# Moving the steps of a slot: places for convolution, attention and routing among the last convolution's products

## The chip, the cores and the metric

The kernel runs on one core of one Trainium2 chip. The metric is the device time of one execution in microseconds, the median of several; lower is better. The core has a matrix engine (TensorE, PE in the profile, with its weight loads as PEld), VectorE (DVE), ScalarE (ACT), GpSimd (POOL), and SyncE (SP), which here only issues transfers. Each engine works off its own list of instructions in order, and the lists meet at semaphores.

## The reference

The model has three parts on an image batch of 8 x 56 x 56 x 256 floats.

```python
# 32 paths: 1x1 convolution to 4 channels, 3x3 convolution, 1x1 back to 256, each with
# batch norm and relu; the paths are summed
paths = jax.vmap(_path, in_axes=(None,) + (0,) * 18)(x, W1, B1, ...)
x = relu(paths.sum(axis=0) + x)
# attention without softmax, per image, on normalised tokens; k and v are normalised per head
kv = einsum('bhnd,bhne->bhde', k, v) / N
out = einsum('bhnd,bhde->bhne', q, kv)
t = t + out + ln(t)
# 8 experts, 2 for each token, over the normalised tokens
logits = tokens @ router_w.T ; rw, re = top_k(softmax(logits), 2)
out = tokens + sum over e of combine[:, e] * (gelu(tokens @ w1[e] + b1[e]) @ w2[e] + b2[e])
```

## The kernel before, in words

The 8 images are cut into 7 chunks each of 448 tokens (8 rows of the image), so there are 56 chunks. The last loop of the kernel walks through 65 slots `s`. In slot `s` several stages of different chunks are worked on side by side, as in a software pipeline:

- the last convolution of chunk `s` (`conv3_steps`): 16 steps of two products. One product (`pair`, L588) is two matmuls into two PSUM banks; ScalarE makes the relu of one bank (L593), VectorE joins the other bank to it (L596). After every second step TensorE sums four of the results over the paths (`sum_paths`, L609).
- the first convolution of chunk `s + 2` (`conv1_steps`): two turns of the input (L249), then the product (L260) whose result ScalarE writes into the image `h1` (L263).
- the second convolution of chunk `s + 1`: `spread_taps` copies shifted rows of `h1` by 12 transfers into `R` (L284); `conv2_steps` has three rows of taps (L298), all into one PSUM bank, and then `halves`, which splits the result in two parts and moves them to `hl` by 16 transfers (L321), the input of the next slot's last convolution.
- the end of chunk `s - 1` (`end_steps`): relu (L644), turn back to tokens (L656), head means (L668), centring on GpSimd (L682), squares on ScalarE (L691), variances on VectorE with a power on GpSimd (L720), inverses on VectorE (L728), scaling on GpSimd (L738), and the head products (L748).
- the attention of chunk `a = s - 8` (`attn_steps`): four matmuls with VectorE work (L874, L878), a power on GpSimd (L892), means (L896), the normalised payload on ScalarE (L903), and its addition and transfer out (`base`, L933 and L935). At the first chunk of an image `image_steps` first makes the tables (L782 and on). `fetch` loads chunk `a + 1` back from DRAM.
- routing of one or two finished chunks (`route_steps`): a series of small VectorE operations with one power on GpSimd (L1010) up to the rows (L1053 to L1062), then 8 scatters for each chunk from GpSimd's queue (L1065). Each scatter waits for the newest product that was written down before it (`pace`), so that the scatters are spread over the slot. From time to time `plan_steps` works out the next tiles of the experts (L1160 to L1213).
- tiles of the experts (`moe_steps`): turn (L1279), first product and gelu (L1321, L1325), second product (L1337, L1341, L1345), and an indirect add into the output from GpSimd (L1359).

Slots 0 to 7 have no attention yet, slots 8 to 55 have all stages except that the expert tiles begin at slot 17, and slots 56 to 64 have only the rest of the attention and the experts.

What a slot's order is, is settled by `issue`. A stage is given as a stretch from `low` to `high` of the slot and a list of steps with costs; each step gets the place where the middle of its cost falls in the stretch. All steps of all stages are sorted by place and written down in that order. The last convolution takes the whole slot, 0 to 1, so that a place is at the same time a place among its products. For TensorE, VectorE and ScalarE the order of writing is the order of execution. Instructions of GpSimd and SyncE are put in order by the framework's scheduler, from the same program.

PSUM tiles of all stages come from one pool of 7 banks in rotation (`ps_mm`); the path sums have the eighth bank.

## Time and profile before

| what | value |
|---|---|
| time, median of 3 | 3348.13 us (3347.52 to 3353.67) |
| profiled run, span | 3349.9 us |
| TensorE busy | 3002.3 us, 90% |
| VectorE busy | 2196.5 us, 66% |
| ScalarE and GpSimd busy | 1900.6 us and 1903.3 us, 57% each |
| mean granted TensorE clock | 0.955 |
| L596 on VectorE | 1792 times, 676 ns each |
| L593 on ScalarE | 1792 times, 636 ns each |
| first product of slot 0 | 58.5 us after the start |
| last product of slot 55 | 2821.0 us |

A row of the profile's groups gives the line, the engine, the operation, what it writes and reads with the shape, how often, busy time and mean; after the bar the idle time of the engine just before these instructions, and what ended most of it. In a timeline a row begins with the start and the duration in microseconds, and the brackets at its end hold the idle time before it and what ended it. An idle engine costs something only where another engine waits for what it was to do.

### The profile page before, as it was taken

To read this page: it belongs to the slowest core of one execution; us is meant where nothing else is said; L and a number is where in the kernel's file an instruction comes from. 1 tells how busy PE (TensorE), PEld (TensorE's weight loads), DVE (VectorE), ACT (ScalarE), POOL (GpSimd) and SP (SyncE) were. 2 spreads that over 40 slices of the span, in tenths; PEclk is the share of its full clock that TensorE was granted. 3 is DMA by queue.
4 is the path that set the end of the run, shared out by engine and by line. 5 is a ranking of instruction groups with operands and counts; after the bars stand their busy time and mean duration, and the time that the engine had idled before them with its cause. 6 is when DMAs were issued, how large, how long until landed. Compare 5 with 4: busy or idle time off the path is not lost. (4 is left out here: it accounts for less than half of the span.)

```text
span 3349.9 us, 55292 instructions
## 1 busy us (share of the span) xinstructions
PE 3002.3 (90%) x16677; PEld 1686.8 (50%) x16677; DVE 2196.5 (66%) x5881; ACT 1900.6 (57%) x3827; POOL 1903.3 (57%) x1372
## 2 busy tenths in 40 slices
PE   5888888888998999999998999999999998798798
PEld 2333433333444554545455555455545545586677
DVE  3666777777777767776776767777777686344300
ACT  2655555645665665566665666566655665354345
POOL 3222234554456466566656566657565666777677
PEclk7999888989999999999998999999999999899999
DMA  6432234435565675666666677566666665798797
GB/s 153 116 87 73 80 111 127 125 108 147 142 163 158 167 189 157 169 161 180 166 167 171 156 196 184 153 177 174 176 164 167 165 168 156 191 267 218 194 220 177
DMA packets 341482, 537.72 MB, mean 161 GB/s; under 512 B 59952, under 2 KB 251584, under 8 KB 341184
## 3 DMA queue, kind: packets, MB, share of 16 engines
q1 hardware_dynamic: 257088, 429.93, 44.1%
q0 software_dynamic: 81984, 103.45, 16.8%
q8 instruction: 134, 2.20, 0.3%
q14 instruction: 164, 1.34, 0.1%
q10 hardware_dynamic: 2112, 0.81, 0.1%
HBM read 248.01 MB, written 192.55 MB: 132 GB/s over the span
## 5 line engine op out<-in xcount | busy, mean ns | idle before, releaser
L596 DVE SCALAR_TENSOR_TENSOR r<-c,nb,r 128x448 f32<-128x448 f32 x1792 | 1127.1, 676 | 563.1 <-ACT r L593 539.7
L593 ACT ACTIVATE r<-c,b3t 128x448 f32<-128x448 f32 x1792 | 1033.1, 636 | 364.1 <-PE c L588 361.7
L1359 POOL DMA_INDIRECT out_dram<-y,index x420 | 662.3, 1577 | 354.0 <-ACT y L1345 251.2
L588 PE MATMUL c<-hl,W3hl 64*128 64x448 f32 x3584 | 708.9, 429 | 74.0 <-ACT r L593 39.6
L609 PE MATMUL su<-r,gather 128*32 128x448 f32 x3584 | 583.7, 577 | 64.0 <-DVE r L596 63.4
L1065 POOL DMA_INDIRECT regions<-pay,rrowi x448 | 431.8, 964 | 316.8 <-PE c L588 202.5
L588 PEld LDWEIGHTS c<-hl,W3hl 64*128 64x128 f32 x3584 | 343.3, 189 | 509.2 <-issue 209.3
L1321 PE MATMUL ph<-eT,w 128*128 128x256 f32 x1680 | 462.1, 406 | 31.5 <-ACT hT L1325 17.1
L1345 ACT ACTIVATE y<-py,g 128x256 f32<-128x256 f32 x420 | 195.4, 474 | 442.2 <-PE py L1341 329.3
L1341 PE MATMUL py<-w,hT 128*128 128x256 f32 x1680 | 436.9, 385 | 0.2
L720 POOL TENSOR_TENSOR hsd<-hsd,half 112x36 f32<-112x36 f32 x56 | 351.5, 6277 | 79.5 <-DVE hsd L719 79.0
L1321 PEld LDWEIGHTS ph<-eT,w 128*128 128x128 f32 x1680 | 302.9, 196 | 172.0 <-issue 65.8
L1325 ACT ACTIVATE hT<-ph,w 128x256 f32<-128x256 f32 x420 | 197.1, 479 | 258.0 <-PE ph L1321 140.9
L1341 PEld LDWEIGHTS py<-w,hT 128*128 128x128 f32 x1680 | 293.4, 193 | 29.8 <-ACT hT L1325 1.4
L682 POOL TENSOR_TENSOR norm<-t,hmean 112x512 f32<-112x512 f32 x112 | 120.3, 1133 | 329.6 <-PE c L588 181.3
L874 PE MATMUL at<-tab,tT 128*112 128x272 f32 x896 | 263.3, 417 | 4.7 <-ACT r L593 4.4
L609 PEld LDWEIGHTS su<-r,gather 128*32 128x32 f32 x3584 | 104.3, 110 | 272.7 <-DVE r L596 155.0
L1337 PE MATMUL py<-b2hl,own 128*128 128x256 f32 x420 | 178.1, 424 | 20.4 <-ACT y L1345 7.1
L874 PEld LDWEIGHTS at<-tab,tT 128*112 128x112 f32 x896 | 147.8, 180 | 83.2 <-issue 16.7
L298 PE MATMUL c<-R,W2t 96*32 96x448 f32 x1344 | 183.2, 573 | 2.9 <-DMA R<-h 1.8
L903 ACT ACTIVATE pay<-X,nm,rs 112x256 f32<-112x256 f32 x224 | 134.9, 604 | 52.6 <-DVE nm L896 52.6
L1010 POOL TENSOR_TENSOR rq<-ebase,rq 112x8 f32<-112x8 f32 (+1 forms) x32 | 53.0, 1656 | 196.1 <-DVE rq L1009 196.1
(255 smaller groups left out, 3196.9 us busy)
## 6 DMA issues: line engine op xcount, KB each, us to landing
w<-Wd SPq DMA_DIRECT2D x210, 513.0 KB
rows<-regions SPq DMA_DIRECT2D x210, 259.0 KB
xi<-in_x_dram SPq DMA_DIRECT2D x56, 448.0 KB
hl<-hi SPq DMA_DIRECT2D x448, 56.0 KB
tTs<-u SPq DMA_DIRECT2D x56, 448.0 KB
ts<-t SPq DMA_DIRECT2D x56, 448.0 KB
tT<-tTs SPq DMA_DIRECT2D x56, 448.0 KB
X<-ts SPq DMA_DIRECT2D x56, 448.0 KB
```

Source lines behind the costliest of these rows:

```text
L588: product = nc.tensor.matmul(tiles[g][:, :CH], W3hl[rows, ab, cg, :], hl[rows, ab, :], start=True, stop=True)
L593: nc.scalar.activation(r, tiles[0][:, :CH], AF.Relu, bias=b3t[:, cg, 2 * ab : 2 * ab + 1])
L596: nc.vector.scalar_tensor_tensor(r, tiles[1][:, :CH], nb3[:, cg, 2 * ab + 1 : 2 * ab + 2], r, op0=ALU.max, op1=ALU.add,)
L609: nc.tensor.matmul(ps[32 * c4 : 32 * c4 + 32, :CH], gather, unit.pop((s, 4 * u + c4)), start=(ab == 0), stop=(ab == NQ - 1),)
L720: nc.gpsimd.tensor_tensor(sd, sd, half[:T, :].rearrange("q (k h) -> q k h", k=KT), ALU.pow)
L874: nc.tensor.matmul(ps, tT[:, f, k * T : (k + 1) * T], tables_of[b][:, f, :], start=(f == 0), stop=(f == NF - 1),)
L1065: ins = nc.gpsimd.indirect_dma_start(out=regions[n], out_offset=bass.IndirectOffsetOnAxis(ap=v["row_i"][:, (m - group[0]) * KT + k, n : n ...
L1321: nc.tensor.matmul(ps, w[:, f * C + hf * P : f * C + (hf + 1) * P], eT[:, f, :], start=(f == 0), stop=(f == NF - 1),)
L1325: nc.scalar.activation(hT[:, hf, :], ps, AF.Gelu, bias=w[:, 2 * NF * C + hf : 2 * NF * C + hf + 1])
L1341: nc.tensor.matmul(ps, hT[:, f, h * P : (h + 1) * P], w[:, (NF + f) * C : (NF + f + 1) * C], start=False, stop=(f == NF - 1),)
L1345: nc.scalar.activation(y[:, h, :], ps, AF.Identity, scale=g[:, h : h + 1])
L1359: ins = nc.gpsimd.indirect_dma_start(out=out_rows, out_offset=at, in_=y[:, h, :], in_offset=None, compute_op=ALU.add, **partial,).ins
```

## The change

Every step of most stages gets a place of its own from a table, in place of the stretch and the costs. The turns of the first convolution move to the slot's start, and its product to half the old place; the taps follow it; the three rows of taps of the second convolution lie together; parts of the attention, of the image tables and of the end of a chunk move by a little. Slots without attention have lists of their own ("alone"), in which the variances come much earlier and the halves later. Routing, scatters and planning keep stretches, with other limits. A step whose place is 1 or more would be carried over to the next slot. The last convolution and the expert tiles keep their stretches. The purpose is that the engines' lists fit each other better; nothing is computed differently.

```diff
+    places = {
+        "attention": [0.108, 0.243, 0.378, 0.514, 0.622, 0.689, 0.744, 0.798, 0.881, 0.881],
+        "attention first": [0.396, 0.487, 0.578, 0.669, 0.742, 0.834, 0.87, 0.907, 0.943, 0.989],
+        "conv1": [0, 0, 0.111],
+        "conv1 alone": [0, 0.011, 0.024],
+        "conv2": [0.615, 0.615, 0.625, 0.675],
+        "conv2 alone": [0.636, 0.642, 0.642, 0.79],
+        "end": [0.109, 0.16, 0.22, 0.251, 0.346, 0.44, 0.56, 0.69, 0.77, 0.917],
+        "end alone": [0.125, 0.16, 0.17, 0.23, 0.31, 0.39, 0.39, 0.64, 0.734, 0.869],
+        "fetch": [0.099],
+        "image": [0.012, 0.118, 0.225],
+        "plan": [0.432, 0.95],
+        "route": [0.016, 0.368],
+        "scatter": [0.302, 0.63],
+        "taps": [0.144],
+        "taps alone": [0.373],
+    }
...
+        era = " alone" if s < A else ""
...
-            work_of.append((0.0, 0.3, conv1_steps(s + 2)))
+            work_of.extend(at("conv1" + era, conv1_steps(s + 2)))
...
-            work_of.append((0.3, 0.36, [(0.0, lambda: spread_taps(s + 1))]))
-            work_of.append((0.5, 0.7, conv2_steps(s + 1)))
+            work_of.extend(at("taps" + era, [(0.0, lambda: spread_taps(s + 1))]))
+            work_of.extend(at("conv2" + era, conv2_steps(s + 1)))
...
-            work_of.append((0.12, 1.0, end_steps(s - 1)))
+            if s < S:
+                work_of.extend(at("end" + era, end_steps(s - 1)))
+            else:
+                work_of.append((0.12, 0.99, end_steps(s - 1)))
...
-            work_of.append((0.2, 0.2, [(0.0, lambda: fetch(a + 1))]))
+            work_of.extend(at("fetch", [(0.0, lambda: fetch(a + 1))]))
...
-                work_of.append((0.0, 0.3, image_steps(a // NCH)))
-            work_of.append((0.35 if opens else 0.05, 0.97, attn_steps(a)))
+                work_of.extend(at("image", image_steps(a // NCH)))
+            if a + A > S:
+                work_of.append((0.35 if opens else 0.05, 0.97, attn_steps(a)))
+            else:
+                work_of.extend(at("attention first" if opens else "attention", attn_steps(a)))
...
-            work_of.append((0.0, 0.35, compute))
+            work_of.append((places["route"][0], places["route"][1], compute))
...
-                work_of.append((0.35, 1.0, scatters[0]))
-                left = [(0.0, 0.65, steps) for steps in scatters[1:]]
+                work_of.append((places["scatter"][0], 0.995, scatters[0]))
+                left = [(0.0, places["scatter"][1], steps) for steps in scatters[1:]]
...
-                work_of.append((0.45, 0.95, plan_steps(closing.index(waiting[-1]))))
+                work_of.append((places["plan"][0], places["plan"][1], plan_steps(closing.index(waiting[-1]))))
```

For the middle of a slot with attention, the old places of the second convolution's steps were 0.525, 0.575, 0.625 and 0.675; those of the end of a chunk 0.125, 0.16, 0.22, 0.28, 0.36, 0.44, 0.56, 0.69, 0.77 and 0.905; those of the first convolution 0.029, 0.087 and 0.208. The products' steps lie at 0.019, 0.106, 0.144, 0.231, 0.269, 0.356, 0.394, 0.481, 0.519, 0.606, 0.644, 0.731, 0.769, 0.856, 0.894 and 0.981 in both.

More of the change, by code (lines that the diff above doesn't have):

```diff
@@ L1394, in moe_steps, with at @@
         return steps
+    places = {
[15 more added lines that the diff above has]
+    }
+    def at(name, steps):
+        out, last = [], 0.0
+        for place, (_, fn) in zip(places[name], steps, strict=True):
+            last = max(last, place)
+            out.append((last, last, [(0.0, fn)]))
+        return out
+    carried = []
     def issue(*parts_of_slot):
-        order = []
+        order = [(p - 1.0, n, fn) for n, (p, fn) in enumerate(carried)]
+        carried.clear()
         for low, high, steps in parts_of_slot:
@@ L1406, in issue @@
             for cost, fn in steps:
-                order.append((low + (high - low) * (at + cost / 2) / total, len(order), fn))
+                p = low + (high - low) * (at + cost / 2) / total
+                if p >= 1.0:
+                    carried.append((p, fn))
+                else:
+                    order.append((p, len(order), fn))
                 at += cost
@@ L1443 @@
             if opens:
-                work_of.append((0.0, 0.3, image_steps(a // NCH)))
-            work_of.append((0.35 if opens else 0.05, 0.97, attn_steps(a)))
+                work_of.extend(at("image", image_steps(a // NCH)))
+            if a + A > S:
+                work_of.append((0.35 if opens else 0.05, 0.97, attn_steps(a)))
+            else:
+                work_of.extend(at("attention first" if opens else "attention", attn_steps(a)))
         work_of.extend(left)
```

## The prediction

> **What bounds the kernel now.** I read the page first, then busy time by stage, then waits by engine, then the timeline of one slot of each kind. A slot is one pass of the last loop: 64 matmuls of L588, so the 3584 of the page are 56 slots, and a slot's edges are the starts of every 64th of them. Stages below are slots 0 to 7 (no attention), 8 to 18 (attention, hardly any expert work), 19 to 55 (all of it), and the tail.
>
> ```profile
> PE 3002.3 (90%) x16677; PEld 1686.8 (50%) x16677; DVE 2196.5 (66%) x5881; ACT 1900.6 (57%) x3827; POOL 1903.3 (57%) x1372
> ...
> 58.50:370.30 311.80, 272.60 (x1472) 116.57 (x1474) 205.35 (x399) 178.48 (x323) 71.64 (x35) 0.92 0.36 99
> 370.30:835.60 465.30, 389.28 (x2152) 177.34 (x2149) 355.40 (x880) 253.98 (x491) 202.77 (x139) 0.92 0.41 119
> 835.60:2821.00 1985.40, 1867.20 (x10702) 1003.15 (x10700) 1460.61 (x3748) 1220.64 (x2450) 1217.45 (x827) 0.98 0.64 167
> 2821.00:3350.00 529.00, 449.12 (x2270) 376.23 (x2268) 159.75 (x805) 241.84 (x556) 386.17 (x279) 0.95 0.85 210
> ...
> 553.00:602.70 49.70, 41.30 (x224) 17.79 (x221) 37.49 (x97) 25.55 (x50) 22.48 (x16) 0.86 0.38 108
> 1096.70:1142.80 46.10, 45.59 (x267) 24.32 (x268) 31.17 (x70) 30.95 (x63) 22.64 (x13) 1.00 0.61 163
> ```
>
> Columns after the length: busy PE, PEld, DVE, ACT, POOL, then PE clock, DMA share, GB/s. TensorE's idle time is length less busy: 39 us, 76 us, 118 us and 80 us. Only this idle time, plus half-clock time, can be won by reordering; the instructions are the same. A plain slot of the third stage (slot 23, last row) has 0.5 us idle: nothing to win there. Slot 12 (the row before) has 8.4 us idle at clock 0.86.
>
> Where slot 12's idle time comes from, by its timeline:
>
> ```profile
> 570.18 2.05 POOL L682 TENSOR_TENSOR norm<-t,hmean 112x512 f32<-112x512 f32 x2 [4.73 <-PE c L588]
> 570.36 0.90 DVE L1053 COPY pay<-rq 112x4 f32<-112x4 f32 x1
> 571.24 1.02 DVE L1055 TENSOR_SCALAR pay<-ids 112x4 int32<-112x4 int32 x1
> 573.83 1.85 PE L609 MATMUL su<-r,gather 128*32 128x448 f32 x4 [2.78 <-DVE r L596]
> ...
> 586.57 0.98 POOL L1065 DMA_INDIRECT regions<-pay,rrowi  x1 [2.68 <-PE c L588]
> 587.58 6.15 POOL L720 TENSOR_TENSOR hsd<-hsd,half 112x36 f32<-112x36 f32 x1
> 593.77 0.19 DVE L728 SCALAR_TENSOR_TENSOR hinv<-hsd 112x32 f32<-112x32 f32 x1 [2.90 <-POOL hsd L720]
> 595.01 2.29 PE L609 MATMUL su<-r,gather 128*32 128x448 f32 x4 [3.14 <-DVE r L596]
> ```
>
> Two chains. First, VectorE does head means and the row block in one run ahead of the next L596, and copies that take 0.16 us elsewhere take 0.90 and 1.02 us beside GpSimd's centring; TensorE's path sum then waits 2.78 us. Second, GpSimd's power (6.15 us) stands behind a scatter that waits for TensorE; VectorE's next step waits 2.90 us for the power, and TensorE 3.14 us for VectorE. The same second wait recurs without a scatter: over the whole run
>
> ```profile
> DVE hinv L728 <- POOL hsd L720: 73.3, 46, 7.8
> PE su L609 <- DVE r L596: 63.4, 39, 3.1
> ```
>
> Third, convolution 2's matmuls lie on both sides of few products: in slot 3
>
> ```profile
> 195.51 0.56 PE L298 MATMUL c<-R,W2t 96*32 96x448 f32 x1 [0.44 <-DMA R<-h]
> 200.09 1.16 ACT L593 ACTIVATE r<-c,b3t 128x448 f32<-128x448 f32 x2 [5.16 <-PE c L588]
> ```
>
> ScalarE got no L588 product for 5.16 us, and VectorE waited with it.
>
> **The Trainium skill.** "PSUM — Partial Sum Buffer", Engine vs sequencer instructions, says that ScalarE, VectorE and GpSimdE queues are strict FIFO and that matmuls keep program order. The trace agrees: the 2.90 us wait above holds every L596 behind it. So a step's place in the program decides. "SBUF — State Buffer", Who interferes with whom, says that VectorE copies and tensor_scalar in a two-port mode block against a GpSimd instruction until it ends. The 0.90 and 1.02 us copies agree. "TensorE: Matmul & The Clock Gate", What's actually happening, says that idle windows halve the matmul clock. The clock column agrees in direction: 0.86 in slot 12, 1.00 in slot 23.
>
> **The change part by part.** No operation is added or removed and no buffer changes; `carried` stays empty, since no place reaches 1. Only orders move.
>
> Slots 0 to 7. (a) Variance goes from 0.56 to 0.39 and inverse from 0.69 to 0.64, so about 9 us lie between (0.25 of 38 us) instead of 5, more than the 6.15 us power. A path-sum gap of 2.25 us before L609 in slots 1, 2, 4, 5, 6, 7 (read off their timelines) goes: -13.5. (b) Means and centring move ahead by about one product step, so the squares no longer hold ScalarE: the 0.81 us gap in slots 1 to 7, -5.7. (c) All of convolution 2 follows product 18; the run of products is more even. Of ScalarE's 5.16 us I count 1 us a slot, -8; the R wait is 0.4. (d) Variance (2.5 us on VectorE, some 0.6 more until the squares are there) now has only two product steps and a path sum (0.67+0.96+0.67 = 2.3 us of TensorE) beside it. Bounded by 0 and 2.5; I take +1.5 a slot, +12. (e) Convolution 1's product comes one product step after the turns: it waits about 0.5 us for ScalarE's copies, +4. (f) Halves at 0.79 start 4.6 us before their first use; the first four transfers need 3.6 us in this trace: nothing, hidden, though thin. Sum -12.
>
> Slots 8 to 18. (a) Means before product 8, rows alone after: the run loses 1.39 us of means and some 1.6 us of stretch, as centring is then over. The 2.78 us gap shrinks by 2.5 in 10, 12, 14, 17, 19: -12.5. (b) In 9, 11, 13, 16, 18 a gap of 1.21 to 2.63 us before the squares shrinks by the 1.2 us that centring is earlier: -6. (c) Convolution 1's product now lies between relu and the first turn of `u`, where TensorE waits 0.74 us in routing slots: -3.7. (d) In the built order of 10, 12, 14, 17 the scatter just ahead of the power is now the fifth, released by product 20, not the fourth, by product 18. The power starts about 2 us later and the inverse keeps its place; queued behind it are the L596 that TensorE needs: +2 in each, +8. (e) Image slots 8 and 15: the first of two waits of 1.9 us for `Arow` has conv 1's turns to hide in, -1 each. Sum -16.
>
> Slots 19 to 55. (a) In 26, 33, 47, 54 the scatter ahead of the power moves up; the power waited to 2750.08 with its input done at 2747.8. An output scatter takes the place, but it could start at 2746.2 and needs 1.6 us. The inverse's wait and the 2.17 us gap go, -8.7. (b) Five image slots, -1 each. (c) The 0.74 us turn wait in seven slots, -5.2. (d) In 24, 28, 52 one more output scatter (1.6 us) precedes the power: +3. (e) The other slots, 0: TensorE is full. Fetch, taps and base move earlier: 0, hidden under whole slots of slack. Sum -16.
>
> Tail: 0; transfers and expert matmuls, in the old order.
>
> The sum is -44. Gaps that end on VectorE come back in part, because it stays the slower side of each product (0.64 against 0.34 us of TensorE). I take two thirds, -29: **3319 us**.
>
> **Rivals.** *All of it counts* and TensorE, less often idle, is granted more clock: -44, and 10 us of the half-clock time in the first two stages (16% of 777 us, 124 us): 3294. For it: each gap has a named cause that the order removes. Against: VectorE's backlog. *Given back*: TensorE full in most of stage three, other gaps merely move: 3347. *Slower*: variance costs its whole 2.5 us and conv 1's product 1 us in eight slots (+28), the power's later start brings half-clock time too (+16), and in three more plan slots VectorE's table block falls beside GpSimd's work as it does here:
>
> ```profile
> 2763.14 2.88 DVE L1209 TENSOR_SCALAR table<-cd 128x14 int32<-128x14 f32 x1
> 2763.81 2.17 POOL L933 TENSOR_TENSOR X<-X,pay 112x1024 f32<-112x1024 f32 x1
> 2766.89 1.84 PE L748 MATMUL kv<-norm 112*128 112x129 f32 x7 [4.39 <-DVE r L596]
> ```
>
> (+13), against -29: +28, 3376. For it: this 4.4 us gap is there in slots 26 and 54 and not in 33 and 47, so alignment alone makes it.
>
> **Chances.** Forecast 0.50, all of it 0.24, given back 0.13, slower 0.13. The range 3284 to 3352 holds the forecast and the given-back case, most of "all of it" (10 us beyond its time) and the near part of "slower". Faster by over 0.2% (6.7 us) 0.76, within 0.11, slower 0.13.
>
> **What would show it.** Right: slots 1 to 7 lose the 2.25 us gap; the L728 wait for L720 falls in stage one and in slots 26, 33, 47, 54 and grows in 10, 12, 14, 17; L1053 and L1055 fall to 0.16 us; clock over 0.92 in the first two stages; slot 23 still 46 us. Wrong: slots 0 to 7 longer than 38.8 us with a new wait behind the variance, a wait for `hl` at a slot's start, or stage three longer than 1985 us.

## The result, and the profile after

The changed kernel takes 3254.86 us (median of 4, 3247.72 to 3258.0) beside 3349.57 us for the kernel before (4 runs, 3347.52 to 3353.67): a ratio of 0.9713 (95% interval 0.9694 to 0.9732), 95 us less. The prediction said 3319 us, 30 us less, with a range from 3284 to 3352. The direction was right, the size three times too small, and the result lies below the range. The profiled run spans 3246.0 us, 103.9 less than the profile of before. It is the quickest of its four runs (3247.72 us), and the profiled run before (3351.62 us) is 2 us over its median, so the sums over slots below add up to 104, not to 95.

The page's busy times of the changed kernel, then busy time by stage (columns as before: the stretch, its length, busy PE, PEld, DVE, ACT and POOL with their counts, PE clock, DMA share, GB/s). The four stages stand first, then slot 12 and slot 23, shown in the prediction for the kernel before:

```profile
PE 2939.6 (91%) x16677; PEld 1679.8 (52%) x16677; DVE 2222.5 (68%) x5881; ACT 1918.3 (59%) x3827; POOL 1900.8 (59%) x1372
```

```profile
57.70:326.00 268.30, 250.61 (x1464) 108.49 (x1464) 207.79 (x399) 180.59 (x323) 71.68 (x35) 0.98 0.41 113
326.00:812.80 486.80, 413.17 (x2372) 195.30 (x2368) 385.11 (x950) 284.50 (x544) 225.21 (x154) 0.92 0.45 128
812.80:2715.30 1902.50, 1797.29 (x10484) 979.45 (x10482) 1456.20 (x3680) 1203.74 (x2396) 1191.67 (x811) 0.98 0.65 171
2715.30:3246.00 530.70, 452.51 (x2270) 381.05 (x2268) 158.00 (x805) 243.73 (x556) 386.96 (x278) 0.93 0.85 209
495.70:544.90 49.20, 40.19 (x222) 18.44 (x220) 36.48 (x97) 25.59 (x49) 22.27 (x16) 0.83 0.35 103
1017.60:1065.60 48.00, 45.84 (x272) 24.32 (x270) 34.41 (x73) 32.15 (x65) 23.81 (x14) 1.00 0.63 162
```

The prediction's second stage ended one slot early: 835.6 is where slot 18 starts, so its second row holds slots 8 to 17 and its third 18 to 55. The rows of the kernel before that fit the second and third row above are:

```profile
370.30:878.80 508.50, 427.97 (x2372) 194.88 (x2369) 386.17 (x948) 282.21 (x545) 225.16 (x154) 0.92 0.42 122
878.80:2821.00 1942.20, 1828.51 (x10482) 985.61 (x10480) 1429.85 (x3680) 1192.40 (x2396) 1195.07 (x811) 0.98 0.64 168
```

The first stage is 43 us shorter (268.3 for 311.8), at clock 0.98 for 0.92. Slots 8 to 18 are 22 us shorter at the clock they had (0.92 for 0.92), slots 19 to 55 40 us shorter. Slot 12 is hardly shorter, and slot 23, where the prediction saw nothing to win, is 1.2 us longer when both profiles are cut in one way (48.0 for 46.8). Cut into kinds of slots, at the start of the last L588 of each, the two profiles read in us:

| slots | before | after | difference |
|---|---|---|---|
| start and slot 0 | 95.9 | 91.5 | -4.4 |
| 1 to 7, no attention | 274.2 | 234.5 | -39.7 |
| 8, 15, 22, 29, 36, 43, 50, which open an image | 436.8 | 403.7 | -33.1 |
| the others from 9 to 19 | 453.2 | 439.7 | -13.5 |
| from 20 on, s modulo 7 = 0 or 3 | 511.0 | 487.2 | -23.8 |
| from 20 on, s modulo 7 = 2, 4 or 6 | 764.7 | 779.4 | +14.7 |
| 26, 33, 40, 47, 54, with plan steps | 285.1 | 279.2 | -6.0 |
| tail | 528.9 | 530.7 | +1.8 |

Seven slots without attention and seven that open an image gave 73 of the 104 us. Part of it is clock. In slots 1 to 7 TensorE's idle time fell from 34.3 to 12.9 us, and its busy time, for the same matmuls, from 239.9 to 221.6. The trace's record of the clock has 34.1 us at half speed there before, and none after. In the seven image slots idle time fell from 65.0 to 48.2 and half-clock time from 92.2 to 54.6 us.

Over the whole run the clock gave less than that, since other slots had more half-clock time than before: the sum fell from 303.8 to 261.0 us. TensorE's idle time fell by 41 us (span less busy time, 347.6 to 306.4), and its busy time by 63 us (3002.3 to 2939.6) for the same 16677 matmuls. Half-clock time, priced at half its length, explains 21 of the 63. What the other 41 us of busy time held is not shown. They aren't all clock: in the slots with s modulo 7 = 0 or 3, where neither profile has any half-clock time, busy time fell by 9.5 us, from 489.5 to 480.0.

How slot 4 gets through its power. From the timeline of the kernel before:

```profile
236.31 6.13 POOL L720 TENSOR_TENSOR hsd<-hsd,half 112x36 f32<-112x36 f32 x1 [6.69 <-DVE hsd L719]
...
242.47 0.19 DVE L728 SCALAR_TENSOR_TENSOR hinv<-hsd 112x32 f32<-112x32 f32 x1 [2.32 <-POOL hsd L720]
...
243.71 2.29 PE L609 MATMUL su<-r,gather 128*32 128x448 f32 x4 [2.25 <-DVE r L596]
```

and of the changed kernel:

```profile
207.53 1.22 DVE L700 TENSOR_REDUCE hss<-sq 112x32 f32<-112x1024 f32 x1 [0.30 <-ACT sq L691]
...
209.35 1.51 PE L588 MATMUL c<-hl,W3hl 64*128 64x448 f32 x3 [0.28 <-ACT r L593]
...
210.10 6.12 POOL L720 TENSOR_TENSOR hsd<-hsd,half 112x36 f32<-112x36 f32 x1 [5.20 <-DVE hsd L719]
...
213.92 2.46 PE L298 MATMUL c<-R,W2t 96*32 96x448 f32 x24
...
216.26 0.19 DVE L728 SCALAR_TENSOR_TENSOR hinv<-hsd 112x32 f32<-112x32 f32 x1 [0.49 <-POOL hsd L720]
...
216.91 0.96 PE L609 MATMUL su<-r,gather 128*32 128x448 f32 x8
```

The power runs from 210.10 to 216.22. VectorE has products to join meanwhile, TensorE has all of convolution 2 (L298, 2.46 us), and the inverse waits 0.49 us. The path sum at 216.91 shows no wait. The variances start at 207.53, and the only gap beside them is 0.28 us.

The waits that the prediction named, over the whole run:

```profile
DVE hinv L728 <- POOL hsd L720: 73.1, 47, 5.9
...
PE su L609 <- DVE r L596: 41.5, 31, 5.1
```

The first sum is as before (73.3), but it has moved. Per slot it falls from about 2.1 us in six of slots 1 to 7 to 0.5 in all seven, and from 2.2 to 0.3 or less in 26, 33, 47 and 54. In 10, 12, 14 and 17 it grows from 2.8 to 4.5. The wait of the path sum fell by 22 us.

### The profile page after: what moved, and what is told of

Read it like the earlier page. It is cut to its first block, busy times and chain, and to the rows that moved or that the text cites. A ratio compares the mean times of both kernels' runs of the same rounds, so it can differ in the third digit from the quotient of the medians.

```text
span 3246.0 us, 55293 instructions
## 1 busy us (share of the span) xinstructions
PE 2939.6 (91%) x16677; PEld 1679.8 (52%) x16677; DVE 2222.5 (68%) x5881; ACT 1918.3 (59%) x3827; POOL 1900.8 (59%) x1372
## 4 chain that ended last, share of the span: by engine, by line
PE 51%; POOL 13%; DVE 11%; issue 8%; DMA 4%; ACT 3%; SPq 0%; POOLq 0%; DVEq 0%; ACTq 0%
PE c L588 9%; PE su L609 9%; PE ph L1321 8%; POOL hsd L720 7%; PE py L1341 7%; PE at L874 5%; DVE r L596 4%; PE kv L748 3%; DMA out_dram<-y,index 3%; POOL out_dram L1359 3%; POOL regions L1065 2%; ACT r L593 2%; PE c L260 2%; PE te L1279 2%; PE py L1337 2%
## 5 line engine op out<-in xcount | busy, mean ns | idle before, releaser
L596 DVE SCALAR_TENSOR_TENSOR r<-c,nb,r 128x448 f32<-128x448 f32 x1792 | 1128.2, 676 | 424.7 <-ACT r L593 379.5
L1359 POOL DMA_INDIRECT out_dram<-y,index x420 | 661.0, 1574 | 329.8 <-ACT y L1345 201.0
L588 PE MATMUL c<-hl,W3hl 64*128 64x448 f32 x3584 | 698.3, 429 | 57.2 <-ACT r L593 25.7
L609 PE MATMUL su<-r,gather 128*32 128x448 f32 x3584 | 565.3, 571 | 41.6 <-DVE r L596 41.5
L588 PEld LDWEIGHTS c<-hl,W3hl 64*128 64x128 f32 x3584 | 329.2, 189 | 527.4 <-issue 231.4
L682 POOL TENSOR_TENSOR norm<-t,hmean 112x512 f32<-112x512 f32 x112 | 126.8, 1259 | 241.4 <-PE c L588 112.9
L1283 ACT COPY eT<-te 128x512 f32<-128x512 f32 x210 | 123.8, 590 | 65.6 <-PE te L1279 63.8
L1279 PE MATMUL te<-ident,rows 128*128 128x128 f32 x840 | 135.1, 285 | 24.2 <-ACT y L1345 23.6
```

What stands on the lines that cost most here:

```text
L588: product = nc.tensor.matmul(tiles[g][:, :CH], W3hl[rows, ab, cg, :], hl[rows, ab, :], start=True, stop=True)
L596: nc.vector.scalar_tensor_tensor(r, tiles[1][:, :CH], nb3[:, cg, 2 * ab + 1 : 2 * ab + 2], r, op0=ALU.max, op1=ALU.add,)
L609: nc.tensor.matmul(ps[32 * c4 : 32 * c4 + 32, :CH], gather, unit.pop((s, 4 * u + c4)), start=(ab == 0), stop=(ab == NQ - 1),)
L1279: nc.tensor.transpose(tp[:, f, h * P : (h + 1) * P], z[:, h, f * P : (f + 1) * P], ident)
L1359: ins = nc.gpsimd.indirect_dma_start(out=out_rows, out_offset=at, in_=y[:, h, :], in_offset=None, compute_op=ALU.add, **partial,).ins
```

## The experiments

All lengths come from one profile each, cut in the same way. The experiments ran on several chips, where the kernel before took 3356 to 3367 us beside them and not 3350. How far one profile can be trusted is seen from profiles with the same steps in the same slots. Slots 1 to 7 agree within 0.1 us in six of them. Slots 9 to 18 without slot 15 gave 389.0, 395.9 and 392.6 us, with 61, 79 and 68 us at half clock, and the seven image slots 391.7 and 399.3. Those with s modulo 7 = 2, 4 or 6 gave 750.4 to 753.9 in four. So in slots 8 to 18 and in the image slots a difference under some 8 us says nothing.

### Putting parts of the change back

The diffs here are against the changed kernel.

**End part of slots 1 to 7, attention of the later slots.**

```diff
-            if s < S:
+            if s < S and s >= A:
                 work_of.extend(at("end" + era, end_steps(s - 1)))
...
-            if a + A > S:
+            if True:
                 work_of.append((0.35 if opens else 0.05, 0.97, attn_steps(a)))
```

> The changed kernel with two parts put back, in different slots: the end part of slots 1 to 7 at its old places, and attention's steps of all later slots at theirs. Slots 1 to 7 took 274.2 us before and 234.5 after. Theory 'distance': the longer way between variance and inverse removed both the 2.25 us wait for the power and the half-clock stretch that followed it, so putting it back costs at least 25 of the 39.7 us (about 262 us). Rival 'evenness': convolution 2 and convolution 1 in one piece each made the products flow; then putting the end part back costs under 12 us (about 245 us, the prediction's own size of its terms for the end part). Later slots: theory 'bunching' says that attention's earlier sums on VectorE made the slots with s modulo 7 = 2, 4, 6 longer by 14.6 us in all (764.8 to 779.4); then they go back to about 765. The rival, that the new convolution and end places do it, leaves them at about 779. Image slots (8 and 15: 108.7 to 97.8; 22 to 50: 328.1 to 306.0): if attention's late places pay, these return to about 109 and 328; if they do not matter they stay.

Slots 1 to 7: 265.4 us, 31 of the 39.7 lost, as "distance" had it. Slot 4 of this kernel, from its timeline:

```profile
230.03 6.12 POOL L720 TENSOR_TENSOR hsd<-hsd,half 112x36 f32<-112x36 f32 x1 [6.68 <-DVE hsd L719]
...
236.19 0.19 DVE L728 SCALAR_TENSOR_TENSOR hinv<-hsd 112x32 f32<-112x32 f32 x1 [3.14 <-POOL hsd L720]
...
237.43 1.53 PE L609 MATMUL su<-r,gather 128*32 128x448 f32 x4 [2.24 <-DVE r L596]
```

The inverse waits 3.14 us where it waited 0.49, and TensorE 2.24 us behind it. Slots 2 and 4 are 37.0 us long without a half-clock window, slots 3 and 6, which have one (6.8 us), 38.9. So the gap isn't always followed by one, and a window of 6.8 us costs about 1.9 us there (2.5 in slot 7), less than half its length. Later slots: s modulo 7 = 2, 4, 6 give 770.1 us, image slots 412.6. Attention's places are part of the 14.7 us lost in the first, and little of the gain in the second.

**The variance alone; the means of the later slots.** In slots 1 to 7 only the last four steps go back, in later slots the whole end part.

```diff
-        "end alone": [0.125, 0.16, 0.17, 0.23, 0.31, 0.39, 0.39, 0.64, 0.734, 0.869],
+        "end alone": [0.125, 0.16, 0.17, 0.23, 0.31, 0.39, 0.56, 0.69, 0.77, 0.905],
...
-            if s < S:
+            if s < S and s < A:
                 work_of.extend(at("end" + era, end_steps(s - 1)))
```

> The changed kernel with, in slots 1 to 7, only variance, inverse, scale and keys-values of the end part put back (0.56, 0.69, 0.77, 0.905), means, centring and squares staying early; in later slots the whole end part at its old places (means at 0.28 and not 0.251, centring 0.36 and not 0.346). 'Distance' in its narrow form, variance against inverse alone: slots 1 to 7 lose what the first kernel of this call loses, within 5 us. If means, centring and squares are what matters, they stay within 8 us of 234.5. Later slots: if the means just ahead of product 8 make the new 2.06 us wait before the weights' load for the head means, slots with s modulo 7 = 2, 4, 6 go from 779.4 back to about 765; the prediction's step for slots 10, 12, 14, 17 and 19 (the rows' 2.78 us wait gone) says that the wait comes back and these slots grow by up to 12.5 us.

Slots 1 to 7: 259.7 us, 25.2 more than with all of the change: 16.5 us of idle time and 8.7 of busy time, with 23.9 us at half clock. The other 5.7 of the 31 us are means, centring and squares. Later slots: those with s modulo 7 = 2, 4, 6 fall to 752.6 us, below the 764.7 of before, while 0 and 3 lose 14.5 of their 23.8 us (501.7). The rows' wait is back in slots 10 and 12 (gaps of 2.65 us), and 10, 12, 14, 17 and 19 take 246.0 for 242.2, not 12.5 more.

The timeline shows why early means cost. Slot 25 of the changed kernel:

```profile
1133.54 1.60 POOL L1359 DMA_INDIRECT out_dram<-y,index  x1 [0.30 <-DVE hmean L671]
...
1134.20 3.07 DVE L1286 COPY g<-rows 128x2 f32<-128x2 f32 x1
1134.57 2.67 POOL L682 TENSOR_TENSOR norm<-t,hmean 112x512 f32<-112x512 f32 x2
...
1137.26 1.26 DVE L596 SCALAR_TENSOR_TENSOR r<-c,nb,r 128x448 f32<-128x448 f32 x2
...
1137.98 1.68 PE L1321 MATMUL ph<-eT,w 128*128 128x256 f32 x4 [2.06 <-DVE r L596]
```

and of this kernel:

```profile
1183.28 0.40 DVE L1286 COPY g<-rows 128x2 f32<-128x2 f32 x1
...
1183.63 1.28 DVE L596 SCALAR_TENSOR_TENSOR r<-c,nb,r 128x448 f32<-128x448 f32 x2
1183.82 2.47 POOL L682 TENSOR_TENSOR norm<-t,hmean 112x512 f32<-112x512 f32 x2
```

An expert tile's copy of 256 numbers takes 3.07 us where centring runs beside it, and ends with it; TensorE's next expert product waits 2.06 us for what stands behind the copy. With the means later the copy is over before centring starts. In the slots with s modulo 7 = 2, 4 or 6, 14 such copies (L1286) took over 1 us in the changed kernel, 11 beside centring and three beside scaling (L738); in the kernel with means by slot below only the three were left, and the kernel before had none. Beside centring L596, which reads PSUM, keeps its 0.64 us a piece. The Trainium skill, "SBUF — State Buffer", Who interferes with whom, says that a copy in a two-port mode and a GpSimd instruction exclude each other: whichever issues first has the ports for its whole length, and the other is blocked. The blocking agrees. Which was first isn't settled here: the copy began 0.37 us before centring, but 0.66 us after the indirect add (L1359), which was still running. Beside that add alone, in the second timeline, the copy took 0.40 us.

**Convolution 2 and taps.**

```diff
-            work_of.extend(at("taps" + era, [(0.0, lambda: spread_taps(s + 1))]))
-            work_of.extend(at("conv2" + era, conv2_steps(s + 1)))
+            work_of.append((0.3, 0.36, [(0.0, lambda: spread_taps(s + 1))]))
+            work_of.append((0.5, 0.7, conv2_steps(s + 1)))
```

> The changed kernel with convolution 2 and the spread of its taps at their old places in every slot. 'Evenness' expects slots 1 to 7 to go from 234.5 us back by 20 or more (to 255 or above), since products and convolution 2 alternate again; the prediction gave this part 8 us; 'distance' expects it to cost under 8 us (below 243). Later slots: with s modulo 7 = 0 and 3 the change gave 12.1 and 11.6 us (254.4 to 242.2, 256.6 to 245.0); if convolution 2 in one piece gave it, they go back to about 254 and 257, else they stay. Image slots: 97.8 and 306.0 stay if image and attention places made their gain.

Slots 1 to 7: 243.1 us, so these steps are worth 8.6. The power stays hidden: in none of these slots does the inverse wait for it. What returns is a path-sum gap of 0.81 us in each, and it stands behind the halves. Slot 4 of this kernel:

```profile
221.62 2.05 POOL L738 TENSOR_TENSOR norm<-norm,hinv 112x512 f32<-112x512 f32 x2 [0.94 <-DVE rs L734]
...
222.69 1.23 DVE L315 CAST hi<-h 128x448 fp32r<-128x448 f32 x1
...
225.23 1.53 PE L609 MATMUL su<-r,gather 128*32 128x448 f32 x4 [0.81 <-DVE r L596]
```

and of the changed kernel:

```profile
217.01 2.06 POOL L738 TENSOR_TENSOR norm<-norm,hinv 112x512 f32<-112x512 f32 x2 [0.79 <-DVE rs L734]
...
221.35 0.38 DVE L315 CAST hi<-h 128x448 fp32r<-128x448 f32 x1
```

At the old place (0.675) the cast that begins the halves (L315) falls beside GpSimd's scaling and takes 1.23 us; at 0.79 the scaling is over, and it takes 0.38. It is so in each of slots 1 to 7, here and in the two kernels below that have the new end part and the old convolution 2 there. So by these traces 5.6 of the 8.6 us come with the halves' later place, and not with the rows of taps lying together; the halves alone weren't put back. Slots with s modulo 7 = 0 and 3: 490.0, they stay. Image slots: 413.4, which is 9.7 more and hardly clear of the noise.

**Convolution 1; the image's steps.**

```diff
-            work_of.extend(at("conv1" + era, conv1_steps(s + 2)))
+            if s % NCH == 1 and s >= A:
+                work_of.extend(at("conv1" + era, conv1_steps(s + 2)))
+            else:
+                work_of.append((0.0, 0.3, conv1_steps(s + 2)))
...
-                work_of.extend(at("image", image_steps(a // NCH)))
+                work_of.append((0.0, 0.3, image_steps(a // NCH)))
```

> The changed kernel with convolution 1 at its old places in all slots that open no image's attention, and in those that do, only the image's own steps (keys, matrix, router) at their old places. Slots 1 to 7: the prediction had convolution 1 at the slot's start cost 4 us, so putting it back would give about 230; 'evenness' has it pay, to 245 or more; 'distance' leaves it within 4 of 234.5. Image slots: theory 'keys first' says that the place of the image's steps made the gain of 33 us (436.8 to 403.8 over the seven), so at least 20 of it goes; the rival, attention's late places or the common parts, leaves them within 7 us of 403.8. Slots with s modulo 7 = 0 and 3: if the hidden wait for the turn (0.74 us in a slot) is what they gained, about half of their 23.7 us returns.

Slots 1 to 7: 239.2 us; convolution 1 at the head of the slot is worth 4.7 us, where the prediction had it cost 4. Image slots: 427.3, so 23.6 of 33.1 us go with the image's places, though the slots around them changed as well. The other later slots say nothing of the change. In them the taps (0.144) now stand ahead of convolution 1's product (0.208), so that they read a row of `h1` before it is written, which changes the input of convolution 2, and ScalarE waits 140.2 us in all at L263 for the taps' transfers (none of that wait in the changed kernel). Most of these slots became longer than before, and the whole profile spans 3390.7 us.

**Routing, scatters and plan steps.**

```diff
-            work_of.append((places["route"][0], places["route"][1], compute))
+            work_of.append((0.0, 0.35, compute))
...
-                work_of.append((places["scatter"][0], 0.995, scatters[0]))
-                left = [(0.0, places["scatter"][1], steps) for steps in scatters[1:]]
+                work_of.append((0.35, 1.0, scatters[0]))
+                left = [(0.0, 0.65, steps) for steps in scatters[1:]]
```

and the plan steps at (0.45, 0.95).

> The changed kernel with routing's steps, scatters and plan steps alone at their old places (0 to 0.35, 0.35 to 1, 0 to 0.65, 0.45 to 0.95). The prediction's step: the scatter that moved ahead of the power in slots 10, 12, 14 and 17 costs 2 us in each (the path-sum gap there went from 3.13 us to 4.54 and 5.08), so these four, 191.4 us after, fall by about 8; in 26, 33, 47 and 54 the power is late again and they grow by up to 8.7; 24, 28 and 52 fall by 3. Rival: the power is late in 10 to 17 because attention's and convolution 2's steps shift what stands ahead of it, and then these four stay within 3 us of 191.4. Slots 1 to 7 (234.5) have no routing and must stay.

Slots 10, 12, 14 and 17: 187.9 us for 191.4, and the inverse waits 4.4 us in each, as in the changed kernel. So routing's own places aren't what made the power late. The first and third experiment say more: with attention's old places the power starts 0.1 us after its input in all four and the inverse waits 1.1 to 2.0 us, and with convolution 2's old places there is no wait in 10, 14 and 17 (4.6 us in 12). The four slots took 187.3 and 190.7 us in these, so the wait isn't what sets their length. In 26, 33, 47 and 54 the wait returns (1.1 us in each), and the plan slots take 284.6, 5.4 more. Slots with s modulo 7 = 0 and 3 lose 10.9 us, so routing's places are part of the gain there; 24, 28 and 52 take 158.1 us, 5.8 more and not 3 less. Those with s modulo 7 = 2, 4 and 6 take 771.5, 7.9 less: they have no half-clock time here and 20.5 us in the changed kernel. Over the whole run nothing can be said of routing's places: the one run took 3252.15 us, beside 3362.49 for the kernel before on its chip.

### Parts of the change alone

The diffs here are against the kernel before, cut to what tells the runs apart.

**End part; later convolutions; image.** The kernel before with the new end part in slots 1 to 7, the new convolutions in later slots that open no image, and the image's places in those that do:

```diff
-            work_of.append((0.0, 0.3, conv1_steps(s + 2)))
+            if s >= A and s % NCH != 1:
+                work_of.extend(at("conv1" + era, conv1_steps(s + 2)))
+            else:
+                work_of.append((0.0, 0.3, conv1_steps(s + 2)))
...
-                work_of.append((0.0, 0.3, image_steps(a // NCH)))
+                work_of.extend(at("image", image_steps(a // NCH)))
```

> The kernel before with one part of the change in each sort of slot: the new end part in slots 1 to 7, the new convolution 1, taps and convolution 2 in later slots that open no image, and in slots that do (8, 15, 22, 29, 36, 43, 50) the new places of the image's own steps. Slots 1 to 7, 274.2 us before: 'distance' expects at most 250 from the end part alone; putting parts back took 31.1 us away for the end part, 8.6 for convolution 2 and taps, 4.8 for convolution 1, so if they add up it gives about 243 to 248. Image slots, 436.8 before: 'keys first' expects 10 to 25 us less; without effect by itself: within 7. Slots with s modulo 7 = 0 and 3 from 20 on, 511.0 before: if the convolutions give the gain there, about 490; if the end part's early means give it, they stay above 505. Slots with s modulo 7 = 2, 4, 6: 764.8 before and no loss here, as means keep their place.

Slots 1 to 7: 249.3, so the end part alone gives 24.9 us. Image slots: 436.0, nothing, a miss. Slots with s modulo 7 = 0 and 3: 510.6, so the convolutions alone give nothing there. Those with 2, 4 and 6: 766.1, no loss, as expected.

**Convolutions in slots 1 to 7; end part in the later ones; attention's late places.**

```diff
-            work_of.append((0.0, 0.3, conv1_steps(s + 2)))
+            if s < A:
+                work_of.extend(at("conv1" + era, conv1_steps(s + 2)))
+            else:
+                work_of.append((0.0, 0.3, conv1_steps(s + 2)))
...
-            work_of.append((0.12, 1.0, end_steps(s - 1)))
+            if A <= s < S:
+                work_of.extend(at("end", end_steps(s - 1)))
+            else:
+                work_of.append((0.12, 1.0 if s < S else 0.99, end_steps(s - 1)))
```

> The kernel before with the other parts: in slots 1 to 7 the new convolution 1, taps and convolution 2 (the end part stays), in later slots the new end part (means at 0.251, centring at 0.346), and in slots that open an image attention's late places. Slots 1 to 7, 274.2 us before: additive parts give 261 to 265; 'evenness' would give 250 or less. Later slots with s modulo 7 = 2, 4, 6: theory 'copy under centring': the early means alone put a 0.2 us copy of an expert tile beside GpSimd's centring, where it takes 3.07 us in slot 25 of the changed kernel, so these go from 764.8 to 775 or more; the rival, that the convolutions' new places are needed too, leaves them below 770. Slots 10, 12, 14, 17 and 19: the rows' wait goes, so 242.1 falls by up to 12.5. Image slots, 436.8: attention's late places and the early means give little, above 425.

Slots 1 to 7: 272.0, 2.2 us from the convolutions alone, against 15 on top of the end part. The parts don't add up: with the old end part the cast L315 takes 0.38 us at its old place too, so moving the halves has nothing to win. Slots with s modulo 7 = 2, 4, 6: 775.4, the number expected, but not from where it was expected. It comes from slots 32, 48 and 55, where a copy beside centring took 1.4 to 1.9 us, while 25, 30 and 37 keep their 47.2 us. In those three, early means alone don't hold the copy up. With all parts new but attention's places (the first experiment) the copy of slot 25 takes 1.14 us, and with all parts new 3.07. Slots 10, 12, 14, 17 and 19: 236.4, which is 5.8 less. Image slots: 446.2, longer than before.

**All of the parts in slots that open an image.**

```diff
+            if s >= A and s % NCH == 1:
+                work_of.extend(at("taps" + era, [(0.0, lambda: spread_taps(s + 1))]))
+                work_of.extend(at("conv2" + era, conv2_steps(s + 1)))
...
+            if s < A or s % NCH == 1:
+                work_of.extend(at("conv1" + era, conv1_steps(s + 2)))
...
-            work_of.append((0.35 if opens else 0.05, 0.97, attn_steps(a)))
+            if a + A > S or not opens:
+                work_of.append((0.35 if opens else 0.05, 0.97, attn_steps(a)))
+            else:
+                work_of.extend(at("attention first", attn_steps(a)))
```

> The kernel before with, in slots that open an image, convolution 1, taps, convolution 2, the image's steps and attention's late places all new (end part and routing old), and in slots 1 to 7 the new end part and convolution 1 (taps and convolution 2 old). Image slots, 436.8 us before and 403.8 after: the image's places alone gave 0.8 and attention's late places none. 'Joint': the keys can only start at the head of the slot when the turns of convolution 1 stand before them, so the parts together give 403 to 412. Rival: the neighbours' new parts are needed, then above 425. Slots 1 to 7, 274.2 before, 249.3 with the end part alone: convolution 1 on top gives 240 to 246 if it was worth the 4.8 us that putting it back cost, and if convolution 2 has to be moved with it, it stays at about 249.

Image slots: 403.2 us, all of the gain, as "joint" had it, with 51.8 us idle and 44.4 us at half clock. Slots 1 to 7: 243.2. Waits of slot 29, first with the image's places alone, then with all parts:

```profile
1378.88 0.79 PE L783 MATMUL sv<-Arow,ones_f 128*128 128x128 f32 x2 [2.02 <-DVE Arow L782]
1381.67 0.80 PE L783 MATMUL sv<-Arow,ones_f 128*128 128x128 f32 x2 [2.00 <-DVE Arow L782]
...
1432.83 0.39 PE L1337 MATMUL py<-b2hl,own 128*128 128x256 f32 x1 [1.45 <-DVE r L596]
...
1436.70 3.67 PE L748 MATMUL kv<-norm 112*128 112x129 f32 x16 [1.49 <-DVE r L596]
```

```profile
1356.16 0.46 PE L783 MATMUL sv<-Arow,ones_f 128*128 128x128 f32 x2 [1.20 <-DVE Arow L782]
1358.73 0.49 PE L783 MATMUL sv<-Arow,ones_f 128*128 128x128 f32 x2 [2.12 <-DVE Arow L782]
...
1404.94 0.39 PE L1337 MATMUL py<-b2hl,own 128*128 128x256 f32 x1 [0.58 <-issue]
...
1408.80 2.36 PE L748 MATMUL kv<-norm 112*128 112x129 f32 x16 [2.01 <-DVE own L1213]
```

With both turns ahead of the keys, one of the two waits shrinks from 2.0 to 1.2 us. A wait of 1.45 us ahead of an expert product falls to 0.58, but the head products wait 2.01 us and not 1.49. This slot has 5.3 us of gaps over 0.6 us instead of 7.0. Half-clock time over the seven slots falls from 95.6 to 44.4 us, so more than half of the 32.8 us between these two kernels is clock (some 26, at half its length). Which of the joint places lifts the clock isn't shown.

### A better kernel, and one that isn't

The first diff is against the changed kernel, the other two build on that version.

**Means by slot.** From slot 20 on the end part's new places only where they paid:

```diff
-            if s < S:
+            if s < S and (s < 20 or s % NCH in (0, 3, 5)):
                 work_of.extend(at("end" + era, end_steps(s - 1)))
```

> A candidate for a better kernel: the changed one, but from slot 20 on the end part's old places (means at 0.28, after the fifth product and not before it) in slots with s modulo 7 = 1, 2, 4 and 6; the others keep the new ones. In the run with the end part old in all later slots those sorts were 26.7 and 4.7 us shorter, and the others longer. 'Copy under centring' expects the sum: slots with s modulo 7 = 2, 4, 6 at about 753 instead of 779.4, image slots 22 to 50 at about 301 instead of 306.0, the others as in the changed kernel (487 for 0 and 3, 279 for 5), 30 us less in all, a span of about 3216. Rival: a slot hands its delay to the next (what one sort gains, its neighbour loses); then the span falls by under 10 us.

Span 3214.6 us. Slots with s modulo 7 = 2, 4, 6 take 750.4 us, image slots 22 to 50 295.5, the others as in the changed kernel: no delay is handed on.

> The kernel with means by slot, timed against the kernel before. The changed kernel stands at 0.9713 of the time before (0.9694 to 0.9732). One profile of this one was 31.4 us shorter than the changed kernel's, with slots 9 to 18 at 395.9 us against 389.0 though they run the same steps there. 'Copy under centring' expects the 26 to 37 us in slots from 20 on to stay: a ratio of 0.960 to 0.964, clear of the changed kernel's interval. The rival, a lucky profile: a ratio within that interval.

3231.52 us (4 runs, 3225.04 to 3235.56) beside 3367.39 for the kernel before on the same chip (7 runs): 0.9596 (0.9577 to 0.9615), clear of the changed kernel's 0.9694 to 0.9732, and in its centre just past what was expected. The second profile has 752.8 us in the slots with s modulo 7 = 2, 4, 6. This version is faster than the kernel before. It was not timed beside the changed kernel itself; that it beats that one too rests on the two ratios.

**The same distance in slots 8 to 18.**

```diff
+        "end sparse": [0.109, 0.16, 0.22, 0.251, 0.346, 0.44, 0.5, 0.77, 0.81, 0.93],
...
-                work_of.extend(at("end" + era, end_steps(s - 1)))
+                work_of.extend(at("end" + (" sparse" if A <= s < 19 else era), end_steps(s - 1)))
```

> The kernel with means by slot (3214.6 us profiled), and in slots 8 to 18 more of the way between variance and inverse: variance at 0.5 instead of 0.56, inverse at 0.77 instead of 0.69, scale at 0.81, keys-values at 0.93. 'Distance', carried over to these slots: the path-sum gaps that end on VectorE behind the power (2.25 us in 9, 11, 13 and 16, 4.4 to 5.1 in 10, 12, 14 and 17, 29 us in all) go, and part of the half-clock windows (92 us in slots 8 to 18) with them: slots 8 to 18, 492.1 us, fall to 450 to 470, a span of 3173 to 3193. Rival: GpSimd's scatters hold the power up wherever it stands, so that it ends later by as much; then the gaps stay or move to the wait for scale and keys-values, and these slots stay above 480.

Slots 8 to 18: 507.3 us for 492.1, the rival's case. VectorE doesn't wait for the power any more, but the wait has moved. Slot 10 of this kernel:

```profile
454.18 0.18 DVE L728 SCALAR_TENSOR_TENSOR hinv<-hsd 112x32 f32<-112x32 f32 x1
454.99 0.94 POOL L1065 DMA_INDIRECT regions<-pay,rrowi  x1 [2.28 <-PE c L588]
456.23 0.94 POOL L1065 DMA_INDIRECT regions<-pay,rrowi  x1 [0.30 <-issue]
457.20 2.06 POOL L738 TENSOR_TENSOR norm<-norm,hinv 112x512 f32<-112x512 f32 x2
458.31 0.50 PEld L748 LDWEIGHTS kv<-norm 112*128 112x128 f32 x2 [2.93 <-POOL norm L738]
458.31 0.80 PE L748 MATMUL kv<-norm 112*128 112x129 f32 x2 [2.65 <-POOL norm L738]
```

The scale now stands behind two paced scatters, and TensorE waits 2.65 us for it at the head products. Half-clock time in slots 8 to 18 rose from 92.2 to 109.2 us.

**The same, with routing of slots up to 18 at its old places.**

```diff
-                work_of.append((places["scatter"][0], 0.995, scatters[0]))
+                work_of.append((0.35, 1.0, scatters[0]) if s < 19 else (places["scatter"][0], 0.995, scatters[0]))
```

and likewise for routing's steps and the second chunk's scatters.

> The first kernel of this call, with routing's steps and scatters of slots up to 18 at their old places (0 to 0.35, 0.35 to 1, 0 to 0.65). Put back alone in the changed kernel this took 5.8 us off slots 9 to 18. If that was the scatters' doing, slots 8 to 18 are 4 to 8 us shorter than in the first kernel; if it was chance in where the half-clock windows fell, within 3 us or longer.

Slots 8 to 18: 508.3, no shorter. So the 5.8 us that routing at its old places had taken off slots 9 to 18 without slot 15 look like chance, and they lie within the noise.

## Why the prediction was right or wrong

**The sum.** The step that failed for the whole is "Only this idle time, plus half-clock time, can be won by reordering", with a forecast that put half-clock time at nothing. The terms came to -44 us of idle time, and idle time did fall by 41. The forecast cut that by a third and stopped there. The busy time, which it took as fixed, fell by 63 us, of which half-clock time explains 21. That -44 and -41 lie so close is luck. In the prediction's first stage idle time fell by 21.5 us (39.2 to 17.7), in slots 8 to 18 by 6.9 (80.5 to 73.6) and in 19 to 55 by 8.5 (113.7 to 105.2), against terms of 12, 16 and 16.

**Slots 0 to 7: right in the main cause, wrong in the sizes.** The prediction's stage sum was -12 (its terms add up to -11.2); slots 1 to 7 gave -39.7, and the start with slot 0 gave -4.4. By putting steps back:

| step | predicted | measured | by |
|---|---|---|---|
| (a) variance and inverse apart | -13.5 | -25.2 | last four steps put back |
| (b) means, centring, squares ahead | -5.7 | -5.7 | the rest of the end part, by difference |
| (c) convolution 2 together, with the taps | -8 | -8.6 | put back |
| (d) variance costs beside two products | +12 | no sign: a 0.28 us gap in slot 4 | timeline |
| (e) convolution 1's product early | +4 | -4.7 | put back |
| (f) halves later | 0 | part of the -8.6 of (c) | the cast L315, 1.23 us when put back and 0.38 in the changed kernel |

They sum to -44.2 and not to -39.7, since the parts overlap. Three steps failed. In (a) the 2.25 us gap was right as idle time (16.5 us measured), but 8.7 us of busy time that go with it, with 23.9 us at half clock, were left out of the forecast and kept for a rival. (d) and (e) were charged at 16 us; the first shows no cost and the second was a gain. That (c) came out at its 8 us is luck: 5.6 us of it belong to the cast of the halves beside GpSimd's scaling, a step that (f) put at nothing, and by the mechanism that the prediction used for the rows.

**Image slots: the largest miss.** "-1 each" became -4.7 each. The step counted one wait for `Arow`, and there it was about right: in slot 29 that wait fell from 1.9 to 1.2 us. It left out the slot's other waits (the table's at L833, 1.47 us before and 0.36 after in slot 29; the head products', 1.48 before and none after) and the clock. Half-clock time over the seven slots fell by 37.6 us, about 19 us of 33. Neither part tried alone makes the gain: the image's places gave 0.8, attention's late places with the early means none, and all together 33.6. The table's wait fell with the image's places alone too, so it isn't what decides; what does stays open.

**Slots 9 to 19 without image: -13.5 against -14 predicted, by luck.** Slots 10, 12, 14, 17 and 19, where (a) and (d) lay, took 242.2 us before and after; all 13.5 us came from 9, 11, 13, 16 and 18, where (b) had 6. The rows' gap of 2.78 us went as predicted, the copies L1053 and L1055 fell from 693 and 434 ns to 226 and 191, and the power's wait grew by 1.7 us in 10, 12, 14 and 17, as (d) had it. It is behind a scatter that the power is late, by 2.3 to 3.3 us where it was 0.5 to 2.4, but routing's new places aren't what put the scatter there: with the old ones the wait is the same, and with attention's old places the power isn't late. In slot 10 it is late by 2.0 us before and 2.3 after; there the growth comes from VectorE, which reaches the inverse 4.1 us after the power's input is done, and not 5.3. The clock didn't rise.

**Slots 20 on without image: -15.1 against -11, by parts that were not foreseen.** (a) The power's wait went in 26, 33, 47 and 54, but in 33 and 47 the wait of the head products behind VectorE's table block appeared (4.43 us at 1574.55 in slot 33), which the prediction knew only in its rival "slower"; the four gave -4.1 and not -8.7. (d) The wait grew from 0.4 to 1.9 us in 24, 28 and 52, yet they became shorter, by 5.9. (c) The 0.74 us wait for the turns stood in ten slots with s modulo 7 = 0 or 3 and is gone, but with the new convolutions alone it fell to 0.24 us and these slots gained 0.4. Of their 23.8 us, 14.5 went when the end part was put back and 10.9 when routing was; by what mechanism isn't shown. "The other slots, 0: TensorE is full" failed both ways. In the slots with s modulo 7 = 2, 4 and 6 the changed kernel lost 14.7 us where copies fell beside centring, a mechanism that the prediction used for the rows and didn't look for in other copies. And full slots can still shrink. Slot 25, L588 alone, in the kernel before and in that with means by slot (length, busy PE, busy PEld):

```profile
1195.40:1242.60 47.20, 11.76 (x68) 5.67 (x64) 1.00 0.76 213
```

```profile
1119.40:1165.20 45.80, 10.75 (x67) 5.01 (x64) 1.00 0.79 214
```

Idle time was 0.5 us in both, and the clock full; the same products take 1.0 us less of busy time. So a busy share of 99% was not the floor. What those products held inside their busy time isn't shown.

**The tail**, 0 predicted, was +1.8. The discount of a third for VectorE's backlog has no support: idle time fell by about the whole sum. Of the rivals, "all of it counts" (3294) was nearest and named the right thing: a TensorE that is less often idle is granted more clock. Its 10 us were too few. In slots 1 to 7 and the image slots 71.7 us of half-clock time went, which at half their length are some 36 us of the 73 gained; elsewhere 29 us came back. The Trainium skill, "TensorE: Matmul & The Clock Gate", HAM oscillation — how this bites in real kernels, prices throttled time at half its length; slots 1 to 7 agree, with 18.3 us of busy time for 34.1 us of half clock, while the single windows of the first experiment cost less than that.

## What to carry to other kernels

Look at what stands between an engine's request and the step that waits for it: the 6.1 us of the power cost a gap of 2.25 us in most of slots 1 to 7 with 0.13 of the slot between variance and inverse, and none with 0.25. Look also at what a moved step then runs beside: rows, expert copies and the cast of the halves each took 0.9 to 3.1 us beside centring or scaling on GpSimd, and 0.2 to 0.4 us away from it. When short gaps of TensorE recur, price them with the half-clock time in the same slots, and don't take TensorE's busy time as fixed. Test a table of places kind of slot by kind of slot: the same early means paid in some slots and cost 1.7 us in each of 16 others (779.4 less 752.8), and splitting them there gave another 1.2%.

## What was not expected of the hardware

Half-clock windows of 3.4 or 6.8 us stood in every one of slots 1 to 7 before, though no gap of TensorE in slot 4 is longer than 2.25 us, and none in slot 3 longer than 0.90; after slot 4's gap at 241.46 the clock fell at 243.8. A gap of the same length in slots 2 and 4 of the first experiment was followed by none. What decides isn't settled here: with the same steps in the same order, slots 9 to 18 without slot 15 had between 61 and 79 us at half clock.

A VectorE copy of 128x2 numbers, 0.2 us by itself on average, took 3.07 us beside an indirect add and two tensor operations on GpSimd, until the second of these ended.
